# Reciprocal rows of an attention's sum: from a POOL copy and a transpose to two products of a repeated column

## The chip, the cores and the metric

The kernel runs on one NeuronCore of a Trainium2 chip. The metric is device time in microseconds (us) of one launch. A profile is one execution recorded by the hardware; its span runs from the first to the last instruction.

## The reference

A block of four parts over x of shape 4 x 1024 x 256, each with a layer norm ahead of it and added to x: a linear recurrent unit, a sparse feed-forward layer with top-32 selection, attention, and the feed-forward layer again. The change lies in the attention:

```python
q = (x @ Wq.T).reshape(b, t, N_HEADS, HEAD_DIM)          # 8 heads of 64
kv_latent = x @ Wkv_down.T                               # 64 wide
k = (kv_latent @ Wk_up.T).reshape(b, t, N_HEADS, HEAD_DIM)
v = (kv_latent @ Wv_up.T).reshape(b, t, N_HEADS, HEAD_DIM)
scores = jnp.einsum('bqhd,bkhd->bhqk', q, k) * scale
attn = jax.nn.softmax(scores, axis=-1)
out = jnp.einsum('bhqk,bkhd->bqhd', attn, v)
return out.reshape(b, t, N_HEADS * HEAD_DIM) @ Wo.T
```

## The kernel before

Everything is in SBUF between the parts. The recurrent unit takes about the first 275 us, with the first steps (`f1.head`) of the first feed-forward layer beside it; that layer's own tiles follow from about 300 us. The long stage of attention follows, from about 390 to 1302 us, in which the rest of the first feed-forward layer and the first steps (`f2.head`) of the second one run beside it; the second feed-forward layer's main part ends the kernel.

In the stage of attention, `heads` (L857) loops over the batch b (4), the half nb (512 queries), the pair of heads g (4 pairs) and the tile q (128 queries, 4 in a half): 128 tiles of 128 queries by 2 heads. For each head j of the pair, TensorE makes the scores `sc` (128 x 1024, L887), VectorE negates them and takes the row's minimum of the negated scores into `pr` and `nm` (L893), ScalarE takes the exp and its sum, `ssum` (L896). The exponents then have to be turned so that the keys lie on the partitions. In tiles with even q this goes by DMA: ScalarE and POOL split them into two f16 parts, `pd` (L899, L900), and the SP queue issues a transposing DMA into `d` (L901). In tiles with odd q TensorE transposes in f32 (`ptp`, L907), and ScalarE or VectorE copies the result to `p` (L912, L910).

`values_sum` (L922) comes later, for a tile whose exponents are turned: lists `pending` and `late` hold it back by a step or more. It takes the reciprocals of the two sums (`rs`, L926), has POOL spread each over 64 columns (`rows`, L928), accumulates the values' products into `po` (L932: the values `la` or `lb` are the stationary operand with 64 columns, head j writes PSUM partitions 64j to 64j + 63; 16 f32 matmuls in a tile with odd q, 48 f16 ones in a tile with even q), transposes `rows` into the second half of `po` (L940), has ScalarE copy that half to `rb` (L942), and has VectorE multiply (L943) into `on`. Each f32 matmul that isn't a transpose is two instructions in the profile, so L932 in f32 shows 32 of them per tile. `output` (L945) multiplies `on` with the output weights.

Three things set the order. `merge` (L965) interleaves the main loop with side work, which has due times written by hand (L1190 to L1215). Pools of buffers: `rs` and `rows` come from a pool with two of each; `po` from PSUM banks with the tag "s", of which there are two, shared with all side work; `d` and `pd` have two, `pr` four. And the framework's planner (`schedule_with_timeline_sim`, L1323) orders the instructions of each engine by its own costs; on the chip each engine then goes through its order, and an instruction that waits holds up what is behind it on that engine.

Of the kernel before, what the change touches and what calls it, by code (L numbers as in the profile page):

```python
# [10 lines left out]
F32 = mybir.dt.float32  # L11
# [10 lines left out]
P = 128  # L22
# [8 lines left out]
HD = 64  # L31
# [742 lines left out]
class Attention:  # L774
# [147 lines left out]
    def values_sum(self, pts, terms, ssum, on, psum):  # L922

        nc, sp = self.nc, self.sp
        rs = sp.tile([P, 2], F32, tag="rs", name="rs")
        nc.vector.reciprocal(rs, ssum)  # L926
        rows = sp.tile([P, 2, HD], F32, tag="rows", name="rows")
        nc.gpsimd.tensor_copy(rows, rs[:, :, None].to_broadcast([P, 2, HD]))  # L928
        po = psum.tile([P, 2, P], "s", "pmo")
        for n, (v, c) in enumerate(terms):  # L930
            for j in range(2):
                nc.tensor.matmul(  # L932
                    po[j * HD : (j + 1) * HD, 0, :],
                    v,
                    pts[j][:, c, :],
                    start=(n == 0),
                    stop=(n == len(terms) - 1),
                )

        nc.tensor.transpose(po[:, 1, :], rows.rearrange("p j d -> p (j d)"), self.ident)  # L940
        rb = sp.tile([P, P], F32, tag="rb", name="rb", bufs=1)
        nc.scalar.copy(rb, po[:, 1, :])  # L942
        nc.vector.tensor_tensor(on, po[:, 0, :], rb, ALU.mult)  # L943
# [383 lines left out]
```

## Time and profile before

| what | value |
|---|---|
| median of three runs | 1528.88 us (1526.93 to 1530.15) |
| the profiled execution's own time | 1528.96 us |
| its span | 1527.2 us |
| mean granted TensorE clock | 0.939 |
| busy over the span: TensorE, VectorE, ScalarE, POOL | 85%, 78%, 67%, 45% |
| L932, TensorE, f32 / f16 | 136.5 us x2048 / 101.6 us x3072 instructions |
| L928, POOL | 37.3 us x128 |
| L940, TensorE, a transpose | x128, 0.328 us each |

Engines: PE is TensorE's matmul, PEld its weight load, DVE VectorE, ACT ScalarE, POOL GpSimd, SP the queue that issues most DMAs. Matmuls are pipelined: the length of one is longer than the distance to the next, so what a stream of them costs is read from start to start. "A <- B" in a list of waits says that A sat idle until B was done; it names the last to come.

### The profile page before, as it was taken

To read this page: it belongs to the slowest core of one execution; us is meant where nothing else is said; L and a number is where in the kernel's file an instruction comes from. 1 tells how busy PE (TensorE), PEld (TensorE's weight loads), DVE (VectorE), ACT (ScalarE), POOL (GpSimd) and SP (SyncE) were. 2 spreads that over 40 slices of the span, in tenths; PEclk is the share of its full clock that TensorE was granted. 3 is DMA by queue.
4 is the path that set the end of the run, shared out by engine and by line. 5 is a ranking of instruction groups with operands and counts; after the bars stand their busy time and mean duration, and the time that the engine had idled before them with its cause. 6 is when DMAs were issued, how large, how long until landed. Compare 5 with 4: busy or idle time off the path is not lost.

```text
span 1527.2 us, 28862 instructions
## 1 busy us (share of the span) xinstructions
PE 1291.6 (85%) x10134; PEld 955.8 (63%) x10136; DVE 1194.9 (78%) x3938; ACT 1025.3 (67%) x2152; POOL 681.6 (45%) x849
## 2 busy tenths in 40 slices
PE   5879998697899888988888988889889999566766
PEld 3635455376677767756776766677777877344544
DVE  8976665697889777779778686877685775599998
ACT  5353433466889767887878777877777876566654
POOL 2033332162555444543544453444353544067775
PEclk9999999699999998999999899999999999679888
DMA  3010000321444343435344333534363445000000
GB/s 118 28 46 15 20 23 21 124 91 60 87 86 95 60 77 73 88 60 86 64 83 78 73 63 70 77 60 84 56 110 72 84 82 100 1 15 25 21 22 32
DMA packets 288612, 96.53 MB, mean 63 GB/s; under 512 B 268233, under 2 KB 284626, under 8 KB 288466
## 3 DMA queue, kind: packets, MB, share of 16 engines
q1 hardware_dynamic: 283024, 88.50, 28.9%
q10 hardware_dynamic: 5442, 6.18, 1.2%
q8 instruction: 80, 1.31, 0.3%
q14 instruction: 66, 0.54, 0.1%
HBM read 16.01 MB, written 11.53 MB: 18 GB/s over the span
## 4 chain that ended last, share of the span: by engine, by line
PE 34%; DVE 34%; ACT 16%; DMA 6%; issue 5%; POOL 4%; SPq 0%; ACTq 0%; POOLq 0%; DVEq 0%
DVE wk L674 8%; PE pmo L932 7%; DVE m L674 6%; PE sc L887 6%; DVE pr L893 6%; ACT pr L896 5%; DMA d<-pd 5%; PE po L437 3%; PE ptp L907 2%; ACT p L912 2%; ACT pd L899 2%; PE pmy L170 2%; PE pu L170 2%; DVE qs L854 2%; PE pz L452 1%
## 5 line engine op out<-in xcount | busy, mean ns | idle before, releaser
L900 POOL TENSOR_TENSOR pd<-pr,pd 128x1024 f16<-128x1024 f32 x128 | 274.3, 2145 | 196.0 <-ACT pd L899 152.1
L893 DVE TENSOR_SCALAR_CACHE_REDUCE pr<-sc 128x1024 f32<-128x1024 f32 x256 | 308.9, 1217 | 60.3 <-POOL pd L900 29.1
L896 ACT ACTIVATE pr<-pr,nm 128x1024 f32<-128x1024 f32 x256 | 294.5, 1152 | 57.2 <-DVE nm L895 38.8
L887 PE MATMUL sc<-kh,qs 128*128 128x512 f32 x512 | 184.4, 438 | 31.6 <-DVE pr L893 16.6
L907 PE MATMUL ptp<-ident,pr 128*128 128x128 f32 x1024 | 144.3, 277 | 24.7 <-ACT p L912 22.3
L887 PE MATMUL sc<-kl,qs 128*128 128x512 f32 x512 | 164.6, 401 | 0.0
L674 DVE MATCH_REPLACE8 wk<-m,wk 128x256 f32<-128x256 f32 x384 | 154.4, 405 | 0.1
L907 PEld LDWEIGHTS ptp<-ident,pr 128*128 128x128 f32 x1024 | 118.3, 142 | 54.2 <-ACT p L912 37.9
L674 DVE MAX8 m<-wk 128x8 f32<-128x256 f32 x384 | 149.9, 410 | 0.6
L912 ACT COPY p<-ptp 128x512 f32<-128x512 f32 x224 | 123.5, 587 | 40.0 <-PE pmo L932 29.8
L899 ACT CAST pd<-pr 128x1024 f16<-128x1024 f32 x128 | 133.6, 1046 | 24.8 <-DMA d<-pd 23.7
L932 PE MATMUL pmo<-p,la 128*64 128x128 f32 x2048 | 136.5, 284 | 4.3 <-DVE qs L854 2.9
L932 PEld LDWEIGHTS pmo<-p,la 128*64 128x64 f32 x2048 | 117.8, 141 | 23.1 <-issue 4.5
L887 PEld LDWEIGHTS sc<-kh,qs 128*128 128x128 f32 x512 | 85.4, 195 | 58.4 <-DVE pr L893 25.4
L628 POOL TENSOR_TENSOR ex<-ex,wk 128x512 f32<-128x512 f32 x61 | 77.9, 1277 | 79.8 <-DVE wk L674 64.9
L887 PEld LDWEIGHTS sc<-kl,qs 128*128 128x128 f32 x512 | 97.3, 191 | 22.7 <-issue 1.0
L932 PE MATMUL pmo<-d,lb 128*64 128x128 f16 x3072 | 101.6, 222 | 7.7 <-ACT ex L615 5.0
L932 PEld LDWEIGHTS <-lb 128*64 128x64 f16 x3072 | 91.4, 111 | 22.2 <-issue 19.0
L928 POOL COPY rows<-rs 128x128 f32<-128x128 f32 x128 | 37.3, 294 | 140.3 <-PE pmo L940 135.6
L699 PE MATMUL pf<-wf,vt 128*128 128x256 f32 x288 | 83.5, 432 | 4.4 <-ACT vt L697 3.6
L147 PE MATMUL pt<-ident,xn 128*128 128x128 f32 x256 | 50.0, 318 | 41.6 <-ACT xn L145 32.9
L556 PE MATMUL pl<-lint,xc_f 128*128 128x512 f32 x128 | 71.8, 648 | 10.4 <-ACT xc_f L587 10.4
(308 smaller groups left out, 2769.9 us busy)
## 6 DMA issues: line engine op xcount, KB each, us to landing
tt<-ft SPq DMA_DIRECT2D x16, 256.0 KB
tt<-tt SPq DMA_DIRECT2D x8, 512.0 KB
out<-x SPq DMA_DIRECT2D x32, 128.0 KB
x<-in_x ACTq DMA_DIRECT2D x6, 512.0 KB
pf<-pfs SPq DMA_DIRECT2D x12, 256.0 KB
full<-pf SPq DMA_DIRECT2D x24, 128.0 KB
d<-pd SPq DMA_TRANSPOSE x128
wa<-in_w_attn SPq DMA_DIRECT2D x2, 640.0 KB
```

What stands on the lines that cost most here:

```text
L556: self.last_logits = nc.tensor.matmul(v, x, w.lint, start=False, stop=True).ins
L628: pool.tensor_tensor(ex, ex, wk, ALU.subtract)
L674: ins = make(*args).ins
L699: nc.tensor.matmul(dst, vt[:, k, :], w.wf[:, k, :], start=(k == 0 and bias is None), stop=(k == KD - 1))
L887: nc.tensor.matmul(sc[:, sl], qs[:, j, q * P : (q + 1) * P], kk[:, sl], start=(i == 0), stop=(i == 1))
L893: nc.vector.tensor_scalar(pr, sc, -1.0, FMAX, ALU.mult, ALU.min, accum_out=nm)
L896: nc.scalar.activation(pr, pr, AF.Exp, bias=nm, scale=-1.0, accum_out=ssum[:, j : j + 1])
L899: nc.scalar.copy(pd[:, 0, :], pr)
L900: nc.gpsimd.tensor_tensor(pd[:, 1, :], pr, pd[:, 0, :], ALU.subtract)
L907: nc.tensor.transpose(pt[:, kk, :], pr[:, kc * P : (kc + 1) * P], self.ident)
L912: nc.scalar.copy(dst, pt)
L932: nc.tensor.matmul(po[j * HD : (j + 1) * HD, 0, :], v, pts[j][:, c, :], start=(n == 0), stop=(n == len(terms) - 1),)
```

## The change

The copy on POOL and its tile `rows` go. The transpose on TensorE goes too; in its place two f32 matmuls take one column of `rs` each, as a view that repeats it 64 times, for the stationary operand, and the identity for the moving one. Output row m of head j is the reciprocal of head j for each of the 128 queries, the same content as before in the same place of `po`. These matmuls write 64 partitions each, as the values' products do. `rs` gets four buffers, where it had the pool's two.

```diff
-        rs = sp.tile([P, 2], F32, tag="rs", name="rs")
+        rs = sp.tile([P, 2], F32, tag="rs", name="rs", bufs=4)
         nc.vector.reciprocal(rs, ssum)
-        rows = sp.tile([P, 2, HD], F32, tag="rows", name="rows")
-        nc.gpsimd.tensor_copy(rows, rs[:, :, None].to_broadcast([P, 2, HD]))
         po = psum.tile([P, 2, P], "s", "pmo")
...
-        nc.tensor.transpose(po[:, 1, :], rows.rearrange("p j d -> p (j d)"), self.ident)
+        for j in range(2):
+            nc.tensor.matmul(
+                po[j * HD : (j + 1) * HD, 1, :],
+                rs[:, j : j + 1].to_broadcast([P, HD]),
+                self.ident,
+                start=True,
+                stop=True,
+            )
         rb = sp.tile([P, P], F32, tag="rb", name="rb", bufs=1)
```

## The prediction

> **What bounds the kernel now.** I read the page first, for the stage: the heads run from about 390 to 1302 us, and everything that is changed lies there. The windows view divides that stage. Its columns are the busy time of each engine with the number of instructions, the granted clock, and what the DMA engines did.
>
> ```profile
> 420.00:640.00 220.00, 199.47 (x2011) 159.17 (x2010) 174.32 (x510) 172.86 (x343) 110.98 (x115) 0.97 0.42 78
> ...
> 860.00:1080.00 220.00, 195.26 (x1930) 154.54 (x1929) 171.39 (x502) 171.07 (x335) 105.50 (x104) 0.98 0.42 75
> ```
>
> TensorE is busy for 91% and 89% of these windows, VectorE and ScalarE for 78%, POOL for half. TensorE is nearest to being the bound, and nothing is saturated. Next, the tile view of `rows` shows what the removed step does.
>
> ```profile
> L928 POOL COPY rows<-rs x128: 279/292/482, 393.0 to 1296.1; 128x128 f32<-128x128 f32 x128
> ...
> L940 PE MATMUL pmo<-ident,rows x128: 327/328/476, 398.8 to 1302.0; 128*128 128x128 f32 x128
> ...
>   PE pmo L940: 135.6, 58
> ...
>   POOL pd L900: 13.1, 8
> ```
>
> POOL copies 128 times at 0.292 us, 37.3 us in all, and stands idle 135.6 us ahead of 58 of these copies: `rows` has two buffers, and the copy for one value product waits for the transpose (L940) of the product two before it. That looks like a large stall, but only where something ready stands behind it does it cost. The view lists 8 cases, 13.1 us, in which `pd` (L900) waited on the copy. Nobody waits for POOL the other way: I paired the 128 copies with the 128 transposes in order of time, and the copy is over at least 2.0 us (median 12 us) before its transpose starts.
>
> Then the chain of waits. I added its pieces over the stage, in twenty windows of 46 us: 943 us, of which TensorE has 315, VectorE 257, ScalarE 193, DMA 84, POOL 30. L928 appears six times, 1.4 us in all; L940 fifty times, 12.9 us. The largest of the six (start, length, what):
>
> ```profile
> 675.79 1.46 PE pmo L932 x48
> 677.25 0.27 PE pmo L940
> 677.58 0.30 POOL rows L928
> 677.88 1.74 SPq L901
> ```
>
> So what POOL gives up is mostly beside the path, and what TensorE takes on is on it about 50 times in 128.
>
> **The TensorE price, step by step.** What the exchange costs is the time from the start of the last product (L932) to the start of whatever follows the reciprocals. The timeline of TensorE (start, length, operation) has every piece of it; merged rows give the last start as start plus length minus one instruction (0.273 us for f32, 0.219 for f16).
>
> ```profile
> 648.25 1.97 PE L932 MATMUL pmo<-p,la 128*64 128x128 f32 x32
> 650.15 0.33 PE L940 MATMUL pmo<-ident,rows 128*128 128x128 f32 x1
> 650.23 0.72 PE L887 MATMUL sc<-kh,qs 128*128 128x512 f32 x2
> ...
> 695.71 0.33 PE L940 MATMUL pmo<-ident,rows 128*128 128x128 f32 x1
> 695.97 1.53 PE L932 MATMUL pmo<-d,lb 128*64 128x128 f16 x48
> 697.43 0.33 PE L940 MATMUL pmo<-ident,rows 128*128 128x128 f32 x1
> 697.60 1.04 PE L907 MATMUL ptp<-ident,pr 128*128 128x128 f32 x8
> ```
>
> In the first three rows the last product starts at 648.25 + 1.97 - 0.27 = 649.95, L940 0.20 later, the scores (L887) 0.08 after that. An f16 product is followed by L940 after 0.15 (695.97 + 1.53 - 0.22 = 697.28, L940 at 697.43). From L940 to the next start: 0.08 to L887 or L170, 0.17 to another transpose (L907) or L554, 0.26 to an operation with 64 columns (L932 again, or L529). So today: after f32 0.29, 0.37 or 0.46 us; after f16 0.23, 0.32 or 0.41.
>
> The new step is two f32 matmuls with 64 columns, each two instructions, so four in place of one. The nearest row is L932 itself: the same shapes, types and the same two halves of the columns. Its 32 instructions start within 1.70 us, 0.055 each: four take 0.22, because the halves run beside each other. Then comes the change of layout to a full-width operation. It too is in the trace, where the planner let scores break into a product:
>
> ```profile
> 1231.95 1.31 PE L932 MATMUL pmo<-p,la 128*64 128x128 f32 x18
> 1233.18 0.73 PE L887 MATMUL sc<-kh,qs 128*128 128x512 f32 x2
> ```
>
> 1231.95 + 1.31 - 0.27 = 1232.99; 0.20 later L887 starts (seven such cases, also before L907, all 0.202 or 0.203). If 64 columns follow, there is no change, and the next pair starts 0.10 later. So afterwards: f32 0.42 (full width) or 0.32; f16 0.35 or 0.25, taking 0.15 for four instructions that need not wait out an f32 pair first (the upper end is the f32 pace, 0.22).
>
> Weighted by what follows L940 in the trace: f32, 27 times L887 or L170 at +0.13, 18 times L907 or L554 at +0.05, 19 times 64 columns at -0.14, together +1.8 us; f16, 24 at +0.12, 31 at +0.035, 6 at -0.16, 3 (L836) at about -0.05, together +2.8. Sum **+4.6 us** of TensorE; with the upper end for f16 64 x 0.07 more, +9.1; if only the 50 of 128 cases on the chain count, 4.6 x 50/128 = +1.8. I take 4.6: TensorE is at 90%, and the waits on other engines lead back to it.
>
> Here two rules of the Trainium skill weigh in. "TensorE: Matmul & The Clock Gate", section Terms, puts a transpose of FP32 at four times the speed of an ordinary one, which speaks against this change: the transposes of L907 start (1.04 - 0.28)/7 = 0.109 us apart, four times that is 0.44 a matmul, 0.87 for both, and the sum would grow by 0.65 x 128 = 83 us, to +88. The row of L932, 0.22 for both, has the same operands' shapes, so it decides. "TensorEngine Tiling (Array Packing)", section Key Properties, says that a change of tiling mode drains the engine: charged alone, it would make the change a gain, since the number of drains is the same before a full-width operation and falls by two 25 times (12 + 7 + 6). The rows agree on the drain but show the four instructions as well; the gain remains only in those 25 cases, and they are in the sum.
>
> **What the trace does not show.** A weight load whose 64 columns are one repeated column. Nearest is the load of `la`, 64 stored columns, 137 ns, hidden behind the matmul before. Below: no gain, since the matmul pair, not the load, sets the 0.10 to 0.11 pace. Above: four loads that no longer hide, 4 x (0.137 - 0.055) = 0.33, x128 = +42 us. I take nothing.
>
> **Removed from POOL, and the reciprocal's new wait.** 37.3 us of copies go; what was directly behind one (7 times `pd`, 8 times L658, 9 others) starts up to 0.35 us earlier or, with the stall, at most 13.1 us in all. I take the chain's 1.4. The stall does not move to TensorE. It could move to VectorE: the slot of `rs` is now freed by TensorE and no longer by the copy, so a reciprocal waits for the product four before it, and the scores' sum (L893) and top-k steps (L674) would be queued behind it, with the exp (L896) waiting for L893. In today's order the reciprocal starts at least 0.39 us (median 5.9) after the transpose four before it, so four buffers cover it: zero. With two it would wait often. The time to a ready `po`, which the copy `rb` (L942) and VectorE's L943 wait for (52.6 us of idle), stays: 0.20 + 0.33 before, 0.22 + 0.27 after. No DMA issue is moved; SP's transposes (L901) wait for L932 and `pd`, both kept.
>
> Sum: 1528.96 for the profiled run (span 1527.2 and 1.8 around it; the median of the runs shown is 1528.88) + 4.6 - 1.4 = **1532.2**, given as 1532.
>
> **Rivals.** (a) Nothing measurable: only the chain's share counts, +1.8 - 1.4, so 1529.4. For it: the chain has TensorE for a third only. Against: its waits come back to TensorE. (b) POOL's stalls were worth what the view lists: -13.1 and +1.8 give 1517.7, half of it 1524. For it: VectorE's L893 waited 29.1 us for `pd` (L900), which reads the four `pr` buffers. Against: only 24 operations stand directly behind a copy, and most were not ready earlier; at 1156.56 POOL had been idle for 5.88 us, yet the chain puts 0.03 us on the copy, as `pd`'s input had just come. (c) Slower by much: the repeated column makes the weight load the pace; it decides once the four starts spread beyond the 0.22 us of L932, and full price is +42, 1571; half, 1550. (d) The planner, which fixes each engine's order by its own costs, orders otherwise: POOL empties earlier, TensorE later in its reckoning, and near ties fall differently. Reciprocals in the trace run a median 20 us ahead of their transpose, though the code has them next to each other, so it does move things. No row prices it; either sign, some 8 us, half a per cent, as an estimate from the single stalls of 2 to 8 us seen on DMA and POOL. That widens every case, to 1544 above.
>
> **How the numbers follow.** A difference under 0.2%, 3 us, can't be told from none. Slower by more: 0.48 (the sum 0.36; a worse order or (c) 0.12). Within: 0.24 (a). Faster: 0.28 (b, or a better order). The likeliest case alone spans 1530 to 1539. The range 1520 to 1544 leaves out the far part of (b) and of (c).
>
> **What would show it.** Right: four L932-like instructions within 0.22 us after each product, 0.20 to the next full-width operation, L928's 135.6 us of POOL idle gone, with POOL's idle ahead of `pd` grown instead, and VectorE waiting for no L932. Wrong: starts wider than 0.055 (c); L893 no longer waiting for `pd` and the stage shorter (b); reciprocals that wait for TensorE; or a stage that differs by far more than 5 us while the local prices hold (d).

## The result and the profile after

| | before | after |
|---|---|---|
| median of six runs, alternating | 1527.64 us (1526.93 to 1530.15) | 1553.62 us (1546.33 to 1556.72) |
| the profiled execution, its span | 1528.96, 1527.2 | 1546.33, 1544.6 |

The change is slower: the ratio is 1.0159, 95% interval 1.0135 to 1.0184, or some 21 to 28 us. The forecast of 1532 had the direction; the size lies outside its range. The profiled execution after is the fastest of its six, so what the trace shows is the low end of the loss: 17.4 us of span. It also had the highest granted clock of the six, 0.946; the slowest, 1556.72 us, had 0.928.

The windows view says where. Its columns are start and end in us, the length, then busy time and instructions of PE, PEld, DVE, ACT and POOL, the granted clock, the DMA share and GB/s. Before, the stage of attention is this window, with 393 us ahead of it and 225 behind:

```profile
393.00:1302.00 909.00, 819.17 (x8334) 652.18 (x8332) 690.15 (x1949) 703.92 (x1356) 427.43 (x417) 0.98 0.43 78
```

After, the last product ends at 1319. This window ends at 1318, with 393 us ahead and 227 behind:

```profile
393.00:1318.00 925.00, 821.41 (x8666) 657.16 (x8664) 699.40 (x1931) 694.89 (x1347) 391.39 (x288) 0.98 0.43 76
```

Nearly all of the loss is in this stage, at the same clock. TensorE is busy 2 us longer in a stage that is 16 longer, so it mostly waits more. POOL has 36 us less to do. VectorE, which the change leaves alone, is busy 9 us longer for 18 instructions fewer: that is the row to be explained.

Next the page's groups. The numbers behind the bar are busy us and mean ns of one, then us idle ahead of the group and what ended most of it. First before:

```profile
PE 1291.6 (85%) x10134; PEld 955.8 (63%) x10136; DVE 1194.9 (78%) x3938; ACT 1025.3 (67%) x2152; POOL 681.6 (45%) x849
...
L900 POOL TENSOR_TENSOR pd<-pr,pd 128x1024 f16<-128x1024 f32 x128 | 274.3, 2145 | 196.0 <-ACT pd L899 152.1
L893 DVE TENSOR_SCALAR_CACHE_REDUCE pr<-sc 128x1024 f32<-128x1024 f32 x256 | 308.9, 1217 | 60.3 <-POOL pd L900 29.1
```

Then after:

```profile
PE 1292.4 (84%) x10518; PEld 961.2 (62%) x10520; DVE 1210.1 (78%) x3938; ACT 1023.1 (66%) x2152; POOL 648.2 (42%) x721
...
L900 POOL TENSOR_TENSOR pd<-pr,pd 128x1024 f16<-128x1024 f32 x128 | 275.2, 2154 | 306.6 <-ACT pd L899 251.3
L893 DVE TENSOR_SCALAR_CACHE_REDUCE pr<-sc 128x1024 f32<-128x1024 f32 x256 | 308.7, 1217 | 61.5 <-POOL pd L900 39.0
```

POOL lost the copies and waits for ScalarE instead, as foretold: 251.3 us ahead of `pd`, where it was 152.1. But VectorE's scores wait longer for POOL, not less: 39.0 us, where it was 29.1.

The new step itself is the tile view of `rs` (the products are now L930, the reciprocals on TensorE L939):

```profile
L939 PEld LDWEIGHTS pmo<-ident,rs x512: 132/137/231, 393.6 to 1319.1; 128*64 128x64 f32 x171
L939 PE MATMUL pmo<-ident,rs x512: 272/273/422, 393.8 to 1319.2; 128*64 128x128 f32 x171
...
  PE pmo L939: 1.4, 2
```

The load of the repeated column takes 137 ns like that of stored columns, and a reciprocal waited for L939 twice, 1.4 us. TensorE's timeline shows the step in its place, once after f16 and once after f32:

```profile
614.21 1.53 PE L930 MATMUL pmo<-d,lb 128*64 128x128 f16 x48
615.58 0.39 PE L939 MATMUL pmo<-ident,rs 128*64 128x128 f32 x4
615.89 0.73 PE L887 MATMUL sc<-kh,qs 128*128 128x512 f32 x2
...
637.46 1.97 PE L930 MATMUL pmo<-p,la 128*64 128x128 f32 x32 [0.82 <-DVE qs L854]
639.25 0.39 PE L939 MATMUL pmo<-ident,rs 128*64 128x128 f32 x4
639.57 0.73 PE L887 MATMUL sc<-kh,qs 128*128 128x512 f32 x2
```

The last f16 product starts at 614.21 + 1.53 - 0.22 = 615.52, the scores 0.37 later; after f32 it is 637.46 + 1.97 - 0.27 = 639.16 and 0.41. The four starts lie within 0.39 - 0.27 = 0.12 us, and the change to full width takes another 0.20. I added what lies between a last product and whatever follows over all 128: about 46 us before, about 52 after. The step costs about 5.9 us at its place. The other 11 us of this run, and some 20 of the medians, are elsewhere.

### The profile page after: what moved, and what is told of

The parts are those of the page before. It is cut to its first block, busy times and chain, and to the rows that moved or that the text cites. A ratio compares the mean times of both kernels' runs of the same rounds, so it can differ in the third digit from the quotient of the medians.

```text
span 1544.6 us, 29460 instructions
## 1 busy us (share of the span) xinstructions
PE 1292.4 (84%) x10518; PEld 961.2 (62%) x10520; DVE 1210.1 (78%) x3938; ACT 1023.1 (66%) x2152; POOL 648.2 (42%) x721
## 5 line engine op out<-in xcount | busy, mean ns | idle before, releaser
L900 POOL TENSOR_TENSOR pd<-pr,pd 128x1024 f16<-128x1024 f32 x128 | 275.2, 2154 | 306.6 <-ACT pd L899 251.3
L893 DVE TENSOR_SCALAR_CACHE_REDUCE pr<-sc 128x1024 f32<-128x1024 f32 x256 | 308.7, 1217 | 61.5 <-POOL pd L900 39.0
L907 PE MATMUL ptp<-ident,pr 128*128 128x128 f32 x1024 | 148.7, 281 | 24.5 <-ACT p L912 23.2
L674 DVE MATCH_REPLACE8 wk<-m,wk 128x256 f32<-128x256 f32 x384 | 157.8, 417 | 0.1
L674 DVE MAX8 m<-wk 128x8 f32<-128x256 f32 x384 | 153.4, 423 | 0.6
L930 PE MATMUL pmo<-p,la 128*64 128x128 f32 x2048 | 133.3, 281 | 8.7 <-DVE qs L854 5.9
L930 PEld LDWEIGHTS pmo<-p,la 128*64 128x64 f32 x2048 | 116.1, 140 | 24.8 <-PE sc L887 5.1
L930 PE MATMUL pmo<-d,lb 128*64 128x128 f16 x3072 | 101.5, 221 | 9.4 <-DVE on L948 5.9
L930 PEld LDWEIGHTS <-lb 128*64 128x64 f16 x3072 | 92.7, 111 | 23.9 <-issue 22.9
L615 ACT ACTIVATE ex<-pl,nm 128x256 f32<-128x256 f32 x128 | 60.3, 471 | 39.0 <-POOL nm L613 37.0
L556 PE MATMUL pl<-lint,xc_f 128*128 128x512 f32 x128 | 75.8, 681 | 10.4 <-ACT xc_f L587 10.4
L699 PE MATMUL pf<-wf,vt 128*128 128x256 f32 x288 | 77.7, 414 | 4.2 <-ACT vt L697 4.0
```

The source lines that it names most:

```text
L556: self.last_logits = nc.tensor.matmul(v, x, w.lint, start=False, stop=True).ins
L674: ins = make(*args).ins
L699: nc.tensor.matmul(dst, vt[:, k, :], w.wf[:, k, :], start=(k == 0 and bias is None), stop=(k == KD - 1))
L893: nc.vector.tensor_scalar(pr, sc, -1.0, FMAX, ALU.mult, ALU.min, accum_out=nm)
L900: nc.gpsimd.tensor_tensor(pd[:, 1, :], pr, pd[:, 0, :], ALU.subtract)
L907: nc.tensor.transpose(pt[:, kk, :], pr[:, kc * P : (kc + 1) * P], self.ident)
```

## The experiments

Two things differ between the kernels: the work, and the order of the rest. Reading each engine's order from the two built programs, and leaving aside what the change adds and removes, 80 of POOL's 717 instructions left the common order, 284 of ScalarE's 1787, 578 of VectorE's 3170 and 752 of TensorE's 8460. So most kernels below have an order written into them: every instruction follows a fixed neighbour on its engine, by an edge that the planner obeys and that makes no wait on the chip. "Old order" is that of before, "new order" that of after.

```diff
+        for a, b in zip(seq, seq[1:]):
+            tc.add_manual_dep(b, a.name,
+                mybir.DependencyInfo(mybir.DependencyClass.NoSync, mybir.DependencyReason.DATA),
+                reason="fixed order")
```

Each kernel was timed beside before, whose medians were 1528.7 to 1529.0 (1529.9 for the last pair). The table of orders shifts the line numbers: the scores' L893 is about L1280 and POOL's L900 about L1287 in these kernels.

**Work or order.** Two controls, and the two mixed kernels. Before with its own order fixed:

> The kernel before, with the order of every engine written down from its own program and pinned by order-only edges between neighbours. A control of the method: both theories say 1528 us, within 0.2% of the kernel before.

1528.71 us, ratio 0.9994 (0.9982 to 1.0007): fixing an order costs nothing that shows. After with its own order fixed:

> The changed kernel with its own order pinned, the second control: both theories say 1547 to 1557 us, as the changed kernel.

1552.56 us, 1.0143 (1.0118 to 1.0169): the whole loss is kept. The change's work in the old order:

> The changed work (no copy on POOL, two products of a repeated column in place of the transpose), with every engine pinned to the order of the kernel before; the two products stand where the transpose stood. Theory A, the planner: what the change itself costs is the predicted few us, the other 20 come from the new order, so 1528 to 1534 us (ratio 1.000 to 1.004). Rival B, the operations: the products, the drains and the missing copy cost the 25 us in any order, so about 1550 us (ratio 1.012 to 1.018).

1539.4 us, 1.0066 (1.0044 to 1.0088). The work alone costs about 10.5 us, and the order another 13.2. The clock doesn't explain the order's part: its median over the executions is 0.9385 in the old order and 0.938 in the new one. The other way round, before's work in the new order, with the copies of POOL placed by the planner:

> The work of the kernel before (copy on POOL and transpose), with TensorE, VectorE, ScalarE, SP and the rest of POOL pinned to the order of the changed kernel; the copies are left to the planner. Theory A: slow although nothing of the change's work is in it, 1544 to 1556 us. Rival B: 1528 to 1532 us.

1562.28 us, 1.0215 (1.0188 to 1.0242), but this holds something else too: with two buffers of `rs`, VectorE's reciprocal waited 19.9 us for POOL's copies, 19 times, which neither kernel does. Again with `rs` in four buffers:

```diff
-        rs = sp.tile([P, 2], F32, tag="rs", name="rs")
+        rs = sp.tile([P, 2], F32, tag="rs", name="rs", bufs=4)
```

> As the kernel before in the new order, but with four buffers for rs, so that a reciprocal no longer waits for the copy before last (19.9 us in the run with two). Theory A, the order costs about 13 us whatever the work: 1541 to 1548 us. If the new order by itself cost 33 us, 1560 us.

1552.61 us, 1.0157 (1.0139 to 1.0175). The new order alone, with none of the change's work, is as slow as the change. Order and work don't add up as they stand: the order costs 13 us on top of the work, or 24 without it; the work costs 10 in the old order and nothing in the new one. Part of this may be the clock. The executions of this last kernel had 0.927 in the median, before beside it 0.937, and a lower clock goes with a longer time: after's six run without exception from 1546.33 us at 0.946 to 1556.72 at 0.928. Over all executions of all kernels, each taken against its own kernel's mean, 0.01 of clock goes with 5.8 us, so by this estimate some 6 of the 24 us go with the clock. Whether the lower clock is a cause or follows from TensorE's waits isn't shown.

**What made the planner choose it.** Three kernels with a free planner. Only the buffers of `rs`:

> The kernel before with one edit, four buffers for rs, and the planner free. No work changes, yet some 320 of VectorE's instructions stand in another place. If the order is a lottery, the time moves by more than 0.2% either way, most likely 1530 to 1545 us; if the order hardly matters, 1528.

1530.92 us, 1.0014 (1.0003 to 1.0025). The copy kept, and two products made from its rows in place of the transpose:

```diff
-        nc.tensor.transpose(po[:, 1, :], rows.rearrange("p j d -> p (j d)"), self.ident)
+        for j in range(2):
+            nc.tensor.matmul(po[j * HD : (j + 1) * HD, 1, :], rows[:, j, :], self.ident, start=True, stop=True)
```

> The planner free; the copy on POOL stays, two products of the copied rows replace the transpose. Its order moves 594 of VectorE's instructions against the kernel before, the changed kernel's 578. If what the planner does with the longer TensorE step is the cause, as slow as the changed kernel or near it, 1545 to 1555 us; if the products cost only their price in a fixed order, 1538.

1556.42 us, 1.0159 (1.0137 to 1.0181). And no copy, with a transpose of the constant identity, so that the normalisation is left out:

```diff
-        nc.gpsimd.tensor_copy(rows, rs[:, :, None].to_broadcast([P, 2, HD]))
...
-        nc.tensor.transpose(po[:, 1, :], rows.rearrange("p j d -> p (j d)"), self.ident)
+        nc.tensor.transpose(po[:, 1, :], self.ident, self.ident)
```

> The planner free; the copy on POOL goes and the transpose turns the constant identity, so that the normalisation is left out. 431 of VectorE's instructions move. In the fixed order this cost 6 us, 1535. If the planner's order is a lottery it lands anywhere from 1525 to 1550; if the missing copy is what the planner answers badly to, 1545 or more.

1533.95 us, 1.0024 (1.0012 to 1.0036). The two products bring a slow order (the same work with before's order fixed takes 1537.73 us, below); the missing copy and the buffers alone don't.

**The two halves of the work, in the old order.** The same two edits with before's order fixed. TensorE's half:

> The order of the kernel before, pinned; the copy on POOL stays, and two products of the copied rows (64 columns each) take the transpose's place: TensorE's part of the change alone. By the prediction's sum the products cost 4.6 us of TensorE, so 1533 us (ratio 1.003). If the products are what costs 10 us in the old order, 1539 us (1.0066), as the whole change in the old order.

1537.73 us, 1.0062 (1.0046 to 1.0079): some 9 us, where 4.6 had been forecast. POOL's half (without normalisation, as above):

> The order of the kernel before, pinned; no copy on POOL, and the one transpose stays but turns the constant identity: the normalisation by the sums is left out, the reciprocals are still made. POOL's part alone. By the prediction 1.4 us less, so 1526 to 1528 us (ratio 0.999); if all POOL waits on the copy counted, 1514; if taking the copy away itself costs, over 1532.

1534.99 us, 1.0052 (1.0034 to 1.0070): about 6 us slower, with runs scattered from 1530.8 to 1540.9, where -1.4 had been forecast. The scatter follows the clock, 0.936 in the fastest and 0.929 in the slowest; at the 5.8 us per 0.01 above, some 4 us would be left. Taking a copy from POOL gains nothing, and seems to cost.

**Where in the order.** From the fixed pair, the starts of the scores compared by their index: the new order gains 2 to 5 us up to about score 20 of 256 (some 435 us), loses about 15 between scores 20 and 84, and is level within 5 us from there. Two more pairs, after against before and before's work in the two orders, have the same course up to score 84, but they lose some 10 us more from there to the end. Only the middle was swapped. The change with the old order except for scores 20 to 84:

> The changed work in the order of the kernel before, except between the scores 20 and 84 of 256 (about 440 to 685 us), where every engine has the new order. If the order's loss sits where the traces part, about 15 us more than the changed work in the old order throughout (1539.4): 1553 to 1556 us. If it is spread over the stage: 1542.

1561.31 us, 1.0217 (1.0202 to 1.0232). The new order except for that middle:

> The complement: the changed work in the new order, except between scores 20 and 84, where it has the old one. If the loss sits there, 1535 to 1539 us, against 1552.6 with the new order throughout; if it is spread, 1549.

1543.06 us, 1.0097 (1.0081 to 1.0112). The middle carries it: -9.5 when it is made old, +21.9 when it is made new. Both came out 4 to 8 us above what was expected; the seams of a mixed order may cost too, which isn't shown. The windows of this middle, first with the change in the old order:

```profile
432.00:670.00 238.00, 214.43 (x2135) 170.67 (x2134) 189.89 (x584) 185.23 (x368) 106.80 (x86) 0.97 0.42 77
```

and then with the change in the new order:

```profile
425.40:681.00 255.60, 222.93 (x2224) 179.76 (x2224) 198.16 (x581) 185.40 (x372) 107.18 (x87) 0.94 0.39 71
```

ScalarE and POOL do the same work in the same time, VectorE needs 8.3 us more for three instructions fewer, and TensorE stands idle for 33 us instead of 24 (it also does 89 instructions more here, which the order moved in from elsewhere). The clock is lower too, 0.94 against 0.97. Full speed is short by 0.06 x 255.6 = 15 us instead of 0.03 x 238 = 7, so at most 8 of the 17.6 us could be that, as an estimate; TensorE's busy time per instruction is the same, 0.100 us.

**What VectorE does in those 8 us.** I took each of its instructions in the stage against the shortest of its own shape. Some are over 0.4 us longer, call them held: 27 with 38.3 us too much in before, 42 with 54.9 in after. In after all 42 end 0.02 or 0.28 us after the end of an instruction on POOL, 26 times the subtraction `pd` (L900). After's timeline has two in a row:

```profile
490.05 2.13 POOL L900 TENSOR_TENSOR pd<-pr,pd 128x1024 f16<-128x1024 f32 x1
490.06 2.13 DVE L64 SCALAR_TENSOR_TENSOR ax_t<-ax_rs 128x4 f32<-128x4 f32 x1
...
490.36 0.27 ACT L947 COPY rb<-pmo 128x128 f32<-128x128 f32 x1
...
492.23 0.16 DVE L65 TENSOR_TENSOR ax_t<-ax_t,ax_v 128x4 f32<-128x4 f32 x1
492.43 0.16 DVE L66 SCALAR_TENSOR_TENSOR ax_rs<-ax_t,ax_rs 128x4 f32<-128x4 f32 x1
492.51 0.28 DVE L948 TENSOR_TENSOR on<-pmo,rb 128x128 f32<-128x128 f32 x1
492.60 2.14 POOL L900 TENSOR_TENSOR pd<-pr,pd 128x1024 f16<-128x1024 f32 x1 [0.42 <-ACT pd L899]
492.71 2.05 DVE L136 SCALAR_TENSOR_TENSOR ax_rs<-ax_mv,ax_rs 128x4 f32<-128x4 f32 x1
492.85 1.70 PE L170 MATMUL pmy<-wvo,onp 128*128 128x256 f32 x12 [1.68 <-DVE on L948]
...
494.80 1.09 ACT L145 ACTIVATE xn<-x,ax_rs 128x256 f32<-128x256 f32 x2 [2.27 <-DVE ax_rs L136]
```

L64 is a step of a layer norm on four columns; L65 and L66, as small, take 0.16 us. Started beside the subtraction it lasts 2.13 us and ends when that ends. L948's input `rb` is ready at 490.63; it starts at 492.51, behind L64, and TensorE has stood for 1.68 us until it is done. Then L136 is caught in the next subtraction, 2.05 us, and ScalarE stands for 2.27. Before has the same thing, fewer times:

```profile
706.88 2.13 POOL L900 TENSOR_TENSOR pd<-pr,pd 128x1024 f16<-128x1024 f32 x1 [0.31 <-ACT pd L899]
707.05 1.99 DVE L66 SCALAR_TENSOR_TENSOR ax_rs<-ax_t,ax_rs 128x4 f32<-128x4 f32 x1
```

In the middle, scores 20 to 84, held time is 7 to 8 us in each kernel whose order there is old, and 13 to 17 where it is new, with before's work as with the change's. In the pair with the change's work the new order holds 9 of the layer norms' small instructions there instead of 4; L636, a step of the feed-forward layer, stays at 5.

**Is the subtraction the cause?** Its place in both orders was given to something else, which writes the same half of `pd` but leaves out the low part of the exponents. First a memset, which reads no SBUF:

```diff
-                    nc.gpsimd.tensor_tensor(pd[:, 1, :], pr, pd[:, 0, :], ALU.subtract)
+                    nc.gpsimd.memset(pd[:, 1, :], 0.0)
```

> The changed work in the old order, with POOL's subtraction for pd (reads two tensors, 2.15 us) replaced by a memset of the same half: the low part of the exponents is left out. VectorE instructions held until a POOL instruction ends were 39.7 us in the stage; 20 of the 31 ended with this subtraction, so they should fall to about 15 us. The time falls too, as POOL has less to do; only the distance to the next run counts.

> The same in the new order. Theory H, VectorE being held by POOL makes up the part of the new order's loss that the held time grew by (14 us of held time in the stage, 8 of them in the middle): the distance to the run in the old order falls from 13 us to 5 or less. Rival, the held time lies beside the path and the loss comes from waits for PSUM banks and values alone: the distance stays at 11 to 15 us.

1518.3 us in the old order, 0.9917 (0.9897 to 0.9937), and 1516.74 in the new one, 0.9912 (0.9893 to 0.9930). The orders, 13.2 us apart with the subtraction, are level. From the page of the new-order run:

```profile
L1289 POOL MEMSET pd<- 128x1024 f16 x128 | 121.1, 951 | 212.5 <-DMA d<-pd 181.9
```

16 instructions are held in either, for 11.7 us (old) and 10.1 (new). But the memset takes 0.95 us in place of 2.15, and no longer keeps `pr`, the exponents' buffer, so that VectorE's wait for `pd` is gone too. To tell these apart, POOL got a copy of the first half, which reads SBUF and also lets `pr` go:

```diff
+                    nc.gpsimd.tensor_copy(pd[:, 1, :], pd[:, 0, :])
```

> The changed work in the old order, with POOL's subtraction for the second half of the split exponents replaced by POOL's copy of the first half (so the low part of the exponents is wrong). POOL still reads SBUF here, one f16 input in place of two of f32 and f16, but it no longer reads the exponents themselves, so their buffer is freed without it, as in the run with the memset. This is the old-order half of a pair; only the distance to the new order counts. I expect a copy of some 1 us, and 1518 to 1530.

> The same edit in the new order. If VectorE is held because POOL reads SBUF, for as long as POOL's instruction lasts: the held instructions stay in number, for about the copy's length each, and the new order stays slower than the old one by the share that the copy has of the subtraction's 2.15 us: some 5 to 7 us of the 13.2 for a copy of 1 us, 10 or more for a copy of 2 us. If the distance between the orders came from the exponents' buffer that waited for POOL, the two orders are as near to each other as with the memset, within 3 us, though VectorE is still held.

The page of the new-order run has the length:

```profile
L1289 POOL COPY pd<-pd 128x1024 f16<-128x1024 f16 x128 | 134.3, 1051 | 377.8 <-ACT pd L1288 336.3
```

1519.51 us in the old order, 0.9933 (0.9911 to 0.9955), 1525.75 in the new one, 0.9976 (0.9963 to 0.9990): 6.2 us apart, from the intervals 3 to 11. Memset and copy are nearly equally long and both leave `pr` alone; the one that reads SBUF brings about half of the distance back, the other none. The copy has 1.05/2.15 = 49% of the subtraction's length and the distance is 6.2/13.2 = 47%; with 3 to 11 us as the interval, so near a match may be luck.

The held time in the traces, one execution each, agrees with this. From the old order to the new one it goes from 39.7 to 53.4 us with the subtraction, from 11.7 to 10.1 with the memset and from 16.1 to 21.6 with the copy (24 and 31 instructions): +13.7, -1.6 and +5.5, beside distances of +13.2, -1.6 and +6.2. VectorE's wait for `pd` doesn't go with the time: it is 29.5 us in the old order and 40.9 in the new one, but 27.9 in the kernel of 1561.31 us and 47.5 in that of 1543.06. So, on the change's work, holding matches the distance between the two orders in size, and `pr` isn't needed for a distance to arise.

Three limits remain. In the swapped middles the match is worse: held time changes by +8.9 us where the time changes by 21.9, and by -11.0 where it changes by -9.5. The copy also waits for ScalarE's half of `pd`, as its row shows and the memset's doesn't; a reading instruction without that wait was not tried. And with before's work, where none of these was tried, held time grows by 8 us only while the new order costs 24.

**A version that beats both?** The new order is 5 us ahead at score 20, so before's work was given that part only, with the old order from there:

> A version to beat both: the work of the kernel before (copy and transpose, four rs buffers), the new order up to score 20, where the traces showed it 5 us ahead, and the old order from there. 1522 to 1526 us (ratio 0.997); if what is gained ahead is lost again behind, 1528 to 1530.

1535.52 us, 1.0035 (1.0018 to 1.0052). And with scores 152 to 162 new as well:

> As the last, with the new order also between scores 152 and 162 (about 945 to 985 us), where it gained 4 us: 1519 to 1523 us (ratio 0.995), or 1528 to 1530 if such gains do not add.

1538.93 us, 1.0072 (1.0058 to 1.0085). Neither holds: the gain in front is given back. No kernel that does the whole work beat before.

## Why the prediction was wrong

- **The step that failed is (d)**: "No row prices it; either sign, some 8 us, half a per cent". The order alone is worth 13 us on the change's work and 24 on before's. It was estimated from single stalls of 2 to 8 us, as if one or two of them could change; an order moves hundreds of instructions, and 15 more of them fell beside POOL's. The mechanism had a row: 27 held instructions with 38.3 us stood in before's trace, up to 2 us each on steps of 0.16. At 1.4 us each (38.3/27), a third of them more or fewer is 13 us: that is where an estimate of this term could have come from, with hindsight. It would still be rough, for it matters where they fall: before's work in the new order has 32 with 46.3 us and is as slow as after.
- **What the hold is.** The Trainium skill has the rule, and the prediction didn't use it: "SBUF — State Buffer", section "SBUF: two separate sides", says that POOL and VectorE share a pair of ports as an exclusive lock, taken for a whole instruction: by a VectorE instruction in a two-port mode, or by one with two SBUF inputs, the latter only against one of POOL that reads SBUF. Traces and runs agree: the held end 0.02 or 0.28 us behind POOL's, and memset against copy is the difference that the rule names. A memset still held 7 instructions in the old order. 5 have one input, so they would have to be in a two-port mode, which no run shows; the 2 with two inputs each started 0.11 us behind one of these and ended with it. That it is the ports is the page's reading; the runs show that the orders differ with an instruction that reads SBUF and waits for ScalarE, and not with one that does neither.
- **TensorE's price, "+4.6 us"**: right at its place. 0.42 and 0.35 us were forecast to the next full-width operation, 0.41 and 0.37 measured, 5.9 in sum. In a fixed order it cost 9 us of the whole (interval 7 to 12). That this is the upper end that was given, 9.1, is chance: it stands on 0.42 after an f16 product, where 0.37 was measured. What adds to it on the way to the end isn't settled.
- **"I take the chain's 1.4" of gain from POOL**: wrong in sign, about 6 us lost in a fixed order, some 4 of them at an equal clock. Eight of the copies stood just ahead of POOL's L658, whose instruction then moves against VectorE: L658 held VectorE 10 times instead of 5, at some 0.6 us each. That can account for 3 us at most; the rest is open.
- **Rival (b)**, stalls given back: no. L893 waits longer for `pd`, and POOL's idle ahead of `pd` grew as foretold. **Rival (c)**, the repeated column as the pace: no, 0.12 us for four starts and 137 ns a load. **Rival (a)**: no. The reciprocal's new wait, taken as zero, is 1.4 us.
- The sign was right, and the work in the old order is slower indeed. That the order went the same way was luck, for it had been given either sign; and the sum foresaw 3.2 us of some 25. The two terms above left out 7 of the rest, the order 13. The prediction's own test for (d), a stage that differs by far more than 5 us while the local prices hold, is what the trace after shows.

## What to carry to other kernels

Where a planner orders the engines, a small change is two changes, its work and a new order; fix the old order under the new work, and the new order under the old work, before explaining either. In the trace of before, look for short VectorE instructions that last as long as a POOL instruction beside them: their number times their loss gives a first size of what a reordering can do, with either sign; here it would have been too small for before's work. The copies taken from POOL gained nothing here, and the same engine's shorter memset gained 21 us: what an engine's time is worth depends on whom its instructions hold or keep waiting, not on its busy share.

## What the hardware showed that was not expected

- A VectorE instruction on 128 x 4 elements lasted up to 2.13 us instead of 0.16 while POOL subtracted; the ends behind POOL's fall on two values, about 0.02 and 0.28 us.
- Giving POOL's subtraction to a memset took 21 us from the change in the old order and 36 in the new one, though POOL is busy for 42% of the span only: its length, its reading, its wait for ScalarE and the buffer it keeps cost others that much, in shares that these runs don't separate.
- f32 products with 64 columns from one repeated column start as fast as from stored ones: four in 0.12 us, 0.20 to the next full-width operation.
